# A second level of block products in the gates of a feed-forward layer

## The chip, the cores and the metric

One kernel on one core of a Trainium2 chip. TensorE (PE; PEld is its weight load), the Vector engine (DVE), ScalarE (ACT), GpSimd (POOL) and the queue engine SyncE (SP) run beside each other and wait for one another by semaphores. The metric is the device time of one execution in microseconds, as the median of several runs.

## What is computed

A decoder layer in f32 on x of 2×512 tokens with 1024 features: a state-space mixer with its own MLP, an attention-like product with quantized codes, and a feed-forward layer. The change is in the feed-forward layer:

```python
def _binary_diff_weight(w, base):
    d = w - base
    coeff = jnp.mean(jnp.abs(d))
    return base + coeff * jnp.sign(d)
W1 = _binary_diff_weight(w1, mean_w1)
W2 = _binary_diff_weight(w2, mean_w2)
W3 = _binary_diff_weight(w3, mean_w3)
gate = jnp.einsum('bsh,ih->bsi', hidden_states, W1)
up = jnp.einsum('bsh,ih->bsi', hidden_states, W3)
h = jax.nn.silu(gate) * up
return jnp.einsum('bsi,hi->bsh', h, W2)
...
x = x + _L0_ffn_ref(_layernorm(x, axis=-1), ...)
```
hidden_states is 1024 tokens × 1024, W1 and W3 are 3584×1024, W2 is 1024×3584.

## The kernel before

Products of matrices are made with seven block products instead of eight (Winograd's form of Strassen's method). For the gates the 3584 rows are cut into 14 groups of 256, and a group is two blocks of 128 rows (of features that come out), two blocks of 512 input features, and two blocks of 512 tokens. A block product is four matmuls of 128×128 weights by 512 tokens. `weight_blocks` makes the left-hand sums of a group's weight (four DVE instructions: s3, a sum in place of a21, s2, s4), `act_blocks` the right-hand ones (t2, t3, t4 and one in place), once for the layer. A `BlockProduct` then runs, for gate or up, on four PSUM banks a to d:

- product 1 into a; ACT copies it to p1
- product 6 into b; DVE: u2 = p1 + b
- product 5 into c, product 4 into d, product 7 onto b; DVE: u3 = p1 + b, c22 = u3 + c
- product 2 onto a (c11); DVE: u3 = u3 + d
- product 3 onto c; DVE: u2 = u2 + c

The four results are the blocks of the group's output. `gates` (L656) runs the groups in turn: gate's product, ACT's Silu of its four blocks, up's product, four DVE multiplications into the hidden tile h, four DVE sums of h's blocks (`hidden_blocks`), one store of h to DRAM (`fhd`). h has one buffer (`hp=1`). The W2 part of a group is brought beside that: `down_blocks` makes four sums in the tile t8 (`fw` in the trace), which is stored too (`fwd`). After the gates, `down` (L712) runs the last projection as seven products over those stores, with 256-column matmuls, and adds to the residual rows (`pairs`, four tiles of 1 MB in SBUF). The small loads `f1a`, `f1b` and so on are its operands; some of them are issued while the gates still run.

W1, W2 and W3 are built on the fly: `ffn_weight` (L1013) loads the sign tile (bf16, SP), ACT scales it (L1029), and a DMA from POOL's queue adds the base to it in SBUF (L1030), three times per group. Signs have been written by an earlier stage. The gates' weights have two buffers, used by odd and even groups.

Groups 0 and 1 begin early: products 1 and 2 of both (`first_products`, L635) need only the first 512 tokens, so `in_turn` puts them between the steps that finish the last 512 tokens (`codes`, `turned`, `product`, `normed`).

The order of the instructions on each engine is fixed when the program is built: a scheduler places them by its own estimate of times, within the bounds of the dependencies; `tc.issue_after(x)` keeps instructions behind x. Each engine runs its own list in order. SP and POOL issue the DMAs, and an issue that has to wait holds up those behind it on that queue.

Of the kernel before, what the change touches and what calls it, by code (L numbers as in the profile page):

```python
# [17 lines left out]
P = 128  # L18
NB = 2
L = 512  # L20
# [17 lines left out]
def decoder(ctx, tc, a, out):  # L38
# [141 lines left out]
    def tiles_waited(**kw):  # L180
        return tc.tile_pool(reuse_waits="tile", **kw)
# [9 lines left out]
    def add(out_, x, y):  # L191
        nc.vector.tensor_tensor(out_, x, y, ALU.add)  # L192

    def sub(out_, x, y):
        nc.vector.tensor_tensor(out_, x, y, ALU.subtract)  # L195
# [28 lines left out]
    def bank(k, name, shape=(P, 512)):  # L224
        return psum.tile(list(shape), F32, tag=f"k{k}", name=name)

    class BlockProduct:


        def __init__(self, places, pl, name, A, B):  # L230
            self.places, self.pl, self.name, self.A, self.B = places, pl, name, A, B
            self.banks = {}
            self.kept = None

        def mm(self, x, i, onto=False):
            if x not in self.banks:
# [18 lines left out]
        def others(self, then=lambda: None):  # L255
            ps = self.banks
            u2, u3, c22 = (self.t(x) for x in ("u2", "u3", "c22"))
            self.mm("b", 6)
            add(u2, self.p1, ps["b"])
            self.mm("c", 5)  # L260
            self.mm("d", 4)
            self.mm("b", 7, True)
            add(u3, self.p1, ps["b"])
            add(c22, u3, ps["c"])
            then()
            add(u3, u3, ps["d"])
            self.mm("c", 3, True)
            self.last = nc.vector.tensor_tensor(u2, u2, ps["c"], ALU.add).ins
            return self.kept if self.kept is not None else ps["a"], u2, u3, c22

        def whole(self):
            self.begin()
# [362 lines left out]
    def first_products(name, act, pl, i, gw, uw):  # L635

        first = {1: act[0][:, :4, :], 2: act[0][:, 4:, :]}
        both = []
        for odd, (x, w) in enumerate((("g", gw), ("u", uw))):
            places = (odd, 2 + odd, 4 + odd, 6 + odd)  # L640
            p = BlockProduct(places, pl, f"{name}{x}{i}", {1: w[:, :4, :P], 2: w[:, 4:, :P]}, first)
            p.weight = w
            if i:
                p.places, p.pl = (2 + 2 * odd,), {"p1": pl["p1b"]}
            both.append(p)

        def c11(p, odd):
            p.c11()
            if i:
                p.kept = pl["c1"].tile([P, L], F32, tag="c", name=f"{p.name}k")  # L650
                nc.scalar.copy(p.kept, p.banks.pop("a"))
                p.places, p.pl = (odd, 2 + odd, 4 + odd, 6 + odd), pl

        return both, [p.begin for p in both] + [lambda p=p, o=o: c11(p, o) for o, p in enumerate(both)]

    def gates(name, act, acts, g, pl, weights, side, begun):  # L656


        dram = [
            [tc.dram_tile([P, 7, 512], F32, name=f"{name}{x}d{i}") for i in range(NG)] for x in ("h", "w")  # L660
        ]
        with g:
            B = act_blocks(name, act, [pl["ap"].tile([P, 4, L], F32, tag=f"t{i}", name=f"{name}t{i}") for i in (2, 3, 4)])
            for i in range(NG):
                gw, uw, t8 = weights(i)
                if i in begun:
# [19 lines left out]
                if not callable(t8):  # L686
                    down_weights(t8, gate.last)
                elif last:
                    down_weights(t8(contexts[0].last), gate.last)
                sg = [gate.t("s")] + list(gc[1:])  # L690
                for o, c in zip(sg, gc):
                    silu = nc.scalar.activation(o, c, AF.Silu).ins
                side(i, pl.get("raw"))
                uc = up.others() if i in begun else up.whole()
                if callable(t8) and not last:
                    down_weights(t8(silu), up.last)
                h = pl["hp"].tile([P, 7, L], F32, tag="h", name=f"{name}h{i}")
                for slot, s_, u_ in zip((0, 3, 1, 2), sg, uc):
                    nc.vector.tensor_tensor(h[:, slot, :], s_, u_, ALU.mult)
# [10 lines left out]
    H, Q = NG // 2, 256  # L710

    def down(name, dram, space, places, finish, work):  # L712

# [141 lines left out]
            ctx_codes(i // 4, i % 4)  # L855

    loaded = [mlp_weights(0)]
    begun, steps = first_products("m", h2T, pl, 0, *loaded[0][:2])
    for step in steps:
        step()  # L860
    dram = gates("m", h2T, acts, g, pl, lambda i: loaded.pop() if loaded else mlp_weights(i), abs_sums, {0: begun})


# [139 lines left out]
                pending.pop(0)()  # L1003

    down("m", dram, 512, (0, 1, 7, 3, 6, 5, 2, 8, 4, 9, 10, 11), ready, work)
    x3T.append(acts.enter_context(tiles_waited(name="x3b", bufs=1)).tile([P, KC, L], F32, name="x3T1"))

    g = ExitStack()
    pl = open_pools(g, "f", ("p1b", "c1", "sp", "ap", "p1", "hp", "t8"))
    g.enter_context(tiles_waited(name="fgap1", bufs=1)).tile([P, 256], F32, name="fgap1")  # L1010
    pl.update(open_pools(g, "f", ("w", "w1")))

    def ffn_weight(i, j, after=None):  # L1013

        n, base = FFN[j]
        if n == "w2":
            to = pl["t8"].tile([P, 8, 512], F32, tag="t8", name=f"fw2{i}")
            dst = to[:, :4, :].rearrange("p a b -> p (a b)")
        else:
            to = pl[("w", "w1")[i % 2]].tile([P, KC, GW], F32, tag="w", name=f"f{n}{i}")  # L1020
            dst = flat(to)
        if "sign" in pl:
            src = pl["sign"].tile([P, KC * GW], BF16, tag="sign", name=f"fs{n}{i}")
# [7 lines left out]
        return to  # L1031

    early = [[ffn_weight(i, j) for j in (0, 1)] for i in (0, 1)]
    traced = nc.cur_bb.bb.instructions
    last = {}

    def in_turn(*parts):
# [9 lines left out]
        return got_  # L1047

    ctx1 = contexts[1]
    begun0, first0 = first_products("f", x3T, pl, 0, *early[0])  # L1050
    begun1, first1 = first_products("f", x3T, pl, 1, *early[1])
    for t in (6, 7):
        ctx1.codes(t)
    in_turn(*first0)
# [4 lines left out]
    pl.update(open_pools(g, "f", ("tmp", "sign")))  # L1059
# [65 lines left out]
```

## Time and profile before

| what | us |
|---|---|
| median of 3 runs | 2484.68 (2483.78 to 2493.46) |
| the profiled execution, its time | 2487.05 |
| its span | 2485.3 |
| first products of groups 0 and 1 begin | 1494.3 |
| their second-stage products begin | 1538.2 |
| gates end, last projection begins | 2184.2 |
| one group of gates | 48.07 |

The span is the time from the first to the last instruction on the core; what lies around it is not in the trace. The profile's page gives busy times by engine; the trace can be asked for the instructions in order of time (the timeline), for stretches of time with the busy time of each engine, and for DMA issues with their time to landing. A matmul's recorded length contains the time for its results to come out, so that neighbours overlap: their pace is read from the distance of their starts. One f32 matmul is two instructions of PE in the trace.

In the gates of this layer the DMA engines are busy 66% of the time at 181 GB/s, ACT 9.2 us and POOL 2.6 us of a group's 48.07.

### The profile page before, as it was taken

To read this page: it belongs to the slowest core of one execution; us is meant where nothing else is said; L and a number is where in the kernel's file an instruction comes from. 1 tells how busy PE (TensorE), PEld (TensorE's weight loads), DVE (VectorE), ACT (ScalarE), POOL (GpSimd) and SP (SyncE) were. 2 spreads that over 40 slices of the span, in tenths; PEclk is the share of its full clock that TensorE was granted. 3 is DMA by queue.
4 is the path that set the end of the run, shared out by engine and by line. 5 is a ranking of instruction groups with operands and counts; after the bars stand their busy time and mean duration, and the time that the engine had idled before them with its cause. 6 is when DMAs were issued, how large, how long until landed. Compare 5 with 4: busy or idle time off the path is not lost.

```text
span 2485.3 us, 20211 instructions
## 1 busy us (share of the span) xinstructions
PE 2438.6 (98%) x7484; PEld 1371.2 (55%) x7492; DVE 1300.0 (52%) x1949; ACT 563.7 (23%) x674; POOL 315.7 (13%) x166
## 2 busy tenths in 40 slices
PE   7999999899999999999999999999999999999999
PEld 5445444444444444445888784444444444488888
DVE  4656676554645556444655654533443343365554
ACT  3222243443324333310000323222112112100000
POOL 1002020522323323210000110000000000000000
PEclk9999999899999999999999999999999999999999
DMA  3110032688888887876856450867576666575651
GB/s 137 36 50 19 28 123 85 241 338 326 337 313 323 350 324 318 324 255 204 249 148 185 134 148 18 217 201 188 151 212 169 163 183 181 165 241 163 210 165 64
DMA packets 174626, 477.50 MB, mean 192 GB/s; under 512 B 20416, under 2 KB 124864, under 8 KB 143552
## 3 DMA queue, kind: packets, MB, share of 16 engines
q1 hardware_dynamic: 167904, 427.98, 47.9%
q0 software_dynamic: 6624, 48.24, 9.9%
q8 instruction: 59, 0.97, 0.2%
q14 instruction: 39, 0.32, 0.0%
HBM read 340.87 MB, written 133.17 MB: 191 GB/s over the span
## 4 chain that ended last, share of the span: by engine, by line
PE 80%; DMA 7%; POOL 4%; DVE 4%; ACT 2%; issue 2%; SPq 1%; POOLq 0%; DVEq 0%; ACTq 0%
DMA smean_w<-in_mean_w 6%; POOL sw L849 3%; PE op L565 2%; ACT sgw L851 1%; PE xa L949 1%; PE dps L349 1%; PE y L485 1%; PE cb L477 1%; DVE down L195 0%; DVE hid L192 0%; PE fo1c L745 0%; PE mo4c L745 0%; PE fo7a L745 0%; PE fo2a L745 0%; PE mo5a L745 0%
## 5 line engine op out<-in xcount | busy, mean ns | idle before, releaser
L849 POOL TENSOR_TENSOR sw<-sw,smean_w 128x2048 f32<-128x2048 f32 x42 | 197.8, 4710 | 403.6 <-DMA smean_w<-in_mean_w 403.6
L851 ACT ACTIVATE sgw<-sw 128x2048 bf16<-128x2048 f32 x42 | 80.2, 1910 | 334.6 <-POOL sw L849 332.1
L1029 ACT ACTIVATE fw<-fsw,coeff 128x2048 f32<-128x2048 bf16 x38 | 75.9, 1997 | 216.7 <-DMA fsw<-sign 45.6
L1030 POOL DMA_DIRECT2D fw<-in_mean_w x42 | 36.2, 861 | 598.7 <-ACT fw L1029 582.8
L853 ACT ACTIVATE sw<-sw 128x2048 f32<-128x2048 f32 x42 | 80.1, 1908 | 0.9
L195 DVE TENSOR_TENSOR down<-down 128x512 f32<-128x512 f32 x56 | 77.6, 1406 | 0.7
L511 POOL TENSOR_TENSOR mz<-mz,ys 128x512 f32<-128x512 f32 x16 | 20.7, 1293 | 309.4 <-DVE ys L508 277.3
L565 PE MATMUL op<-wout,mz 128*128 128x512 f32 x128 | 56.6, 592 | 0.0
L91 POOL TENSOR_TENSOR q_r<-q_e,mhalf 128x1 f32<-128x1 f32 x8 | 6.5, 807 | 259.7 <-DVE q_e L87 259.1
L565 PEld LDWEIGHTS op<-wout,mz 128*128 128x128 f32 x128 | 23.9, 190 | 27.7 <-issue 27.5
L195 DVE TENSOR_TENSOR fw<-fw 128x512 f32<-128x512 f32 x56 | 37.1, 683 | 0.1
L118 PE MATMUL h1T<-ident,h 128*128 128x128 f32 x64 | 15.2, 383 | 16.6 <-ACT h L340 10.7
L195 DVE TENSOR_TENSOR mh<-mh 128x512 f32<-128x512 f32 x42 | 28.8, 686 | 0.5
L195 DVE TENSOR_TENSOR fh<-fh 128x512 f32<-128x512 f32 x42 | 28.7, 682 | 0.1
L949 PE MATMUL xa<-c,c1T 128*128 128x512 bf16 x122 | 28.1, 379 | 0.5 <-ACT c1T L937 0.2
L192 DVE TENSOR_TENSOR hid<-hid,op 128x512 f32<-128x512 f32 x24 | 15.9, 683 | 23.8 <-PE op L565 23.8
L349 PEld LDWEIGHTS dps<-wdt,h1T 128*128 128x128 f32 x128 | 23.7, 272 | 2.4 <-issue 1.8
L161 ACT ACTIVATE cc<-ctx,back 128x2048 bf16<-128x2048 f32 x8 | 16.0, 1996 | 27.1 <-DVE ctx L160 27.1
L349 PE MATMUL dps<-wdt,h1T 128*128 128x8 f32 x128 | 22.1, 301 | 0.0
L584 POOL TENSOR_TENSOR hid<-hid,xa 128x1024 f32<-128x1024 f32 x8 | 20.4, 2558 | 11.7 <-DMA xa<-in_x 9.1
L118 PEld LDWEIGHTS h1T<-ident,h 128*128 128x128 f32 x64 | 12.1, 223 | 17.1 <-ACT h L340 10.7
L952 DVE SCALAR_TENSOR_TENSOR hid<-xa,s,hid 128x512 f32<-128x512 f32 x16 | 12.0, 749 | 17.8 <-PE xa L949 17.7
(1979 smaller groups left out, 5300.8 us busy)
## 6 DMA issues: line engine op xcount, KB each, us to landing
sw<-in_w SPq DMA_DIRECT2D x42, 1024.0 KB, 7.7
smean_w<-in_mean_w SPq DMA_DIRECT2D x42, 1024.0 KB, 9.2
fw<-in_mean_w POOLq DMA_DIRECT2D x42, 1024.0 KB, 10.6
mwd<-down SPq DMA_DIRECT2D x14, 1792.0 KB, 7.2
fwd<-fw SPq DMA_DIRECT2D x14, 1792.0 KB, 8.9
mhd<-mh SPq DMA_DIRECT2D x13, 1792.0 KB, 7.0
fhd<-fh SPq DMA_DIRECT2D x13, 1792.0 KB, 10.3
sign<-sgw SPq DMA_DIRECT2D x42, 512.0 KB, 3.0
```

Source lines behind the costliest of these rows:

```text
L118: nc.tensor.transpose(ps[:, i, :], src[:, k * P : (k + 1) * P], ident)
L195: nc.vector.tensor_tensor(out_, x, y, ALU.subtract)
L349: nc.tensor.matmul(dps[:, t, :], h1T[t // TPB][:, k, c : c + P], wdt[:, k, :], start=(k == 0), stop=(k == KC - 1))
L477: nc.tensor.matmul(cb, o["B"][:, cols], o["C"][:, :, cols], start=True, stop=True)
L485: nc.tensor.matmul(y, o["xt"][:, c, :], att, start=True, stop=(c == 0))
L565: nc.tensor.matmul(ps, A[p][:, k, t * P : t * P + P], B[p][:, k, :], start=(k == 0), stop=(k == 3))
L849: nc.gpsimd.tensor_tensor(w, w, b, ALU.subtract)
L851: nc.scalar.activation(sg, w, AF.Sign)
L853: nc.scalar.activation(w, w, AF.Abs, accum_out=sums[:, j, i : i + 1])
L949: nc.tensor.matmul(ps, self.c1T[:, k, c : c + P], self.c2[k // 4][:, k % 4, hs], start=(k == 0), stop=(k == KC - 1))
L1029: nc.scalar.activation(dst, src, AF.Identity, scale=coeff[:, j : j + 1])
L1030: nc.gpsimd.dma_start(dst, a[base][i].rearrange("p a b -> p (a b)"), accum_op=ALU.add)
```

## The change

Products 1 and 2 of gate and up share their right-hand sides, and so do 6 and 7. Gate and up are now taken as two row blocks of one product, the 512 input features as 2×256 and the 512 tokens as 2×256, and the same seven-product form is applied once more inside (`second_level`). One call does two of the outer products together: an index q of 2 stands for product 1 and 2 (or 6 and 7), whose results lie beside each other in one bank. Each inner product is four matmuls of 256 columns. The sums for the inner level are made by `second_level_right` (once per layer and pair) and `second_level_left` (per group and pair). The outer products 3, 4 and 5 stay as they were (`one`), for gate and up.

The combination of the outer products is done by additions over gate and up together, on results in SBUF. Groups 0 and 1 take products 1 and 2 in the plain form (`first_two`), as these begin early. The tiles for the right-hand sums of the inner level (`places`, three of 1 MB) and for the signs take the place of the residual rows, which are written to DRAM (`xd`) before the gates and read back (`xf`) after them.

```diff
-    POOLS = dict(t8=1, w=2, w1=2, raw=2, ap=1, sp=2, hp=1, tmp=7, p1=2, p1b=2, c1=2, sign=2)
+    POOLS = dict(t8=1, w=2, w1=2, raw=2, ap=1, sp=2, hp=1, tmp=7, p1=2, o12=2, o67=1, px=2, s23=1, s4=2, y12=1, y67=1)
...
+    def second_level_right(b, t2, t3, t4):
+        b11, b12, b21, b22 = (b[:, :, k : k + 2, c : c + Q] for k in (0, 2) for c in (0, Q))
+        sub(t3, b22, b12)
+        sub(b12, b12, b11)
+        sub(t2, b22, b12)
+        sub(t4, b21, t2)
+        return {1: b11, 2: b21, 3: b22, 4: t4, 5: b12, 6: t2, 7: t3}
+
+    def second_level_left(g_, u_, s1, s2, s3, s4):
+        a11, a12, a21, a22 = g_[:, :, :2], g_[:, :, 2:], u_[:, :, :2], u_[:, :, 2:]
+        sub(s3, a11, a21)
+        add(s1, a21, a22)
+        sub(s2, s1, a11)
+        sub(s4, a12, s2)
+        return {1: a11, 2: a12, 3: s4, 4: a22, 5: s1, 6: s2, 7: s3}
+
+    def second_level(name, banks, p1, A, B, O):
+        ps = {x: bank(k, f"{name}{x}", (P, 2, Q)) for x, k in zip("abcd", banks)}
+        def mm(x, i, onto=False):
+            for q in range(2):
+                for k in range(2):
+                    nc.tensor.matmul(
+                        ps[x][:, q, :], A[i][:, q, k, :], B[i][:, q, k, :],
+                        start=not onto and q == 0 and k == 0, stop=k == 1, skip_group_check=onto or q > 0,
+                    )
+        c11, u2, u3, c22 = (O[:, :, x, c : c + Q] for x in (0, 1) for c in (0, Q))
+        mm("a", 1)
+        nc.scalar.copy(p1, ps["a"])
+        mm("b", 6)
+        add(u2, p1, ps["b"])
+        mm("c", 5)
+        mm("d", 4)
+        mm("b", 7, True)
+        add(u3, p1, ps["b"])
+        add(c22, u3, ps["c"])
+        mm("a", 2, True)
+        nc.scalar.copy(c11, ps["a"])
+        add(u3, u3, ps["d"])
+        mm("c", 3, True)
+        add(u2, u2, ps["c"])
...
+            for i in range(NG):
...
+                if i in begun:
+                    O12 = begun[i]
+                else:
+                    O12 = pl["o12"].tile([P, 2, 2, L], F32, tag="o", name=f"{name}o12_{i}")
+                    p1 = pl["px"].tile([P, 2, Q], F32, tag="p", name=f"{name}p12_{i}")
+                    second_level(f"{name}m{i}", X, p1, A12, B12, O12)
+                    add(O12[:, 1], O12[:, 0], O12[:, 1])
+                w2 = t8(None)
+                if i == 0:
+                    c, d = one("c", 5), one("d", 4)
+                p1 = pl["px"].tile([P, 2, Q], F32, tag="p", name=f"{name}p67_{i}")
+                O67 = pl["o67"].tile([P, 2, 2, L], F32, tag="o", name=f"{name}o67_{i}")
+                second_level(f"{name}n{i}", Y, p1, A67, B67, O67)
+                add(O67[:, 0], O12[:, 0], O67[:, 0])
+                turn = nc.vector.tensor_tensor(O67[:, 1], O67[:, 0], O67[:, 1], ALU.add).ins
+                if i:
+                    c = one("c", 5)
+                for j in range(2):
+                    add(O12[:, 0, j], O67[:, 1, j], c[j])
+                if i:
+                    d = one("d", 4)
+                for j in range(2):
+                    add(O67[:, 1, j], O67[:, 1, j], d[j])
+                one("c", 3, True)
+                coming.pop(0)
+                if not last:
+                    with tc.issue_after(turn):
+                        if i + 1 not in begun:
+                            A12 = outer_left(i + 1, *coming[0][:2])
+                        A, A67 = left(i + 1, *coming[0][:2])
+                if i == 0:
+                    b = act[0].rearrange("p (q k) l -> p q k l", q=2)
+                    B12 = second_level_right(b, ex[1][:, 1], ex[2][:, 0], ex[2][:, 1])
+                if i + 2 < NG:
+                    coming.append(weights(i + 2))
+                with tc.issue_after(turn):
+                    down_blocks(w2)
+                nc.sync.dma_start(dram[1][i], w2[:, 1:, :])
+                for j in range(2):
+                    add(O67[:, 0, j], O67[:, 0, j], c[j])
+                h = pl["hp"].tile([P, 7, L], F32, tag="h", name=f"{name}h{i}")
+                for slot, o in ((0, O12[:, 1]), (2, O12[:, 0]), (1, O67[:, 1]), (3, O67[:, 0])):
+                    nc.scalar.activation(o[:, 0], o[:, 0], AF.Silu)
+                    nc.vector.tensor_tensor(h[:, slot, :], o[:, 0], o[:, 1], ALU.mult)
...
+    xd = tc.dram_tile([P, NT // 2, 2 * D], F32, name="xd")
+    places = []
+    for j in range(NT // 2):
+        with tc.issue_after(loads):
+            nc.sync.dma_start(xd[:, j, :], flat(pairs[j]))
+        if j < 3:
+            places.append(xpool.tile([P, 2, D], F32, tag=f"x{2 * j}", name=f"ft{j}"))
+        else:
+            two = xpool.tile([P, 2, KC * GW], BF16, tag=f"x{2 * j}", name="fsign")
+            sign_places.extend(two[:, k, :] for k in range(2))
...
-    dram = gates("f", x3T, acts, g, pl, ffn_weights, lambda i, wp: None, {0: begun0, 1: begun1})
-    down("f", dram, 14464, (9, 10, 11, 3, 0, 1, 4, 2, 5, 6, 7, 8), store, lambda: None)
+    dram = gates2("f", x3T, acts, g, pl, ffn_weights, {0: begun0, 1: begun1}, places)
+    for j in range(NT // 2):
+        pairs[j] = xpool.tile([P, 2, D], F32, tag=f"x{2 * j}", name=f"xf{2 * j}")
+        nc.sync.dma_start(flat(pairs[j]), xd[:, j, :])
+    down("f", dram, 14336, (9, 10, 11, 4, 2, 3, 5, 8, 0, 1, 6, 7), store, lambda: None)
```
`left` makes the outer sums of a group's weights, as `weight_blocks` did, and from them the inner ones of 6 and 7 (3 sums in one new tile and one in place); `outer_left` makes the inner sums of 1 and 2. L832 of the changed kernel is the addition called `turn`. `loads` is the last load that the first `down` issues on SP.

More of the change, by code (lines that the diff above doesn't have):

```diff
@@ L232, in __init__ @@
             self.banks = {}
-            self.kept = None
         def mm(self, x, i, onto=False):
@@ L268, in others @@
             self.last = nc.vector.tensor_tensor(u2, u2, ps["c"], ALU.add).ins
-            return self.kept if self.kept is not None else ps["a"], u2, u3, c22
+            return ps["a"], u2, u3, c22
         def whole(self):
@@ L633, in open_pools, with first_products @@
         return pl
-    def first_products(name, act, pl, i, gw, uw):
+    def first_products(name, act, pl, gw, uw):
         first = {1: act[0][:, :4, :], 2: act[0][:, 4:, :]}
@@ L639, in first_products @@
         for odd, (x, w) in enumerate((("g", gw), ("u", uw))):
-            places = (odd, 2 + odd, 4 + odd, 6 + odd)
-            p = BlockProduct(places, pl, f"{name}{x}{i}", {1: w[:, :4, :P], 2: w[:, 4:, :P]}, first)
+            p = BlockProduct((odd, 2 + odd, 4 + odd, 6 + odd), pl, f"{name}{x}0", {1: w[:, :4, :P], 2: w[:, 4:, :P]}, first)
             p.weight = w
-            if i:
-                p.places, p.pl = (2 + 2 * odd,), {"p1": pl["p1b"]}
             both.append(p)
-        def c11(p, odd):
+        for p in both:
+            p.begin()
+        for p in both:
             p.c11()
[L649 to L654, printed above, removed]
+        return both
     def gates(name, act, acts, g, pl, weights, side, begun):
@@ L684, in down_weights @@
                     nc.sync.dma_start(dram[1][i], t8[:, 1:, :])
[L686 to L689, printed above, removed]
+                down_weights(t8, gate.last)
                 sg = [gate.t("s")] + list(gc[1:])
                 for o, c in zip(sg, gc):
-                    silu = nc.scalar.activation(o, c, AF.Silu).ins
-                side(i, pl.get("raw"))
+                    nc.scalar.activation(o, c, AF.Silu)
+                side(i, pl["raw"])
                 uc = up.others() if i in begun else up.whole()
-                if callable(t8) and not last:
-                    down_weights(t8(silu), up.last)
                 h = pl["hp"].tile([P, 7, L], F32, tag="h", name=f"{name}h{i}")
@@ new lines, in first_two, with step @@
+    def first_two(name, act, pl, i, gw, uw, banks):
+        O = pl["o12"].tile([P, 2, 2, L], F32, tag="o", name=f"{name}o12_{i}")
+        ps = []
+        def step(p, x, w):
+            if not p:
+                ps.append(bank(banks[x], f"{name}a{x}_{i}"))
+            for k in range(4):
+                nc.tensor.matmul(
+                    ps[x], w[:, 4 * p + k, :P], act[0][:, 4 * p + k, :],
+                    start=not p and k == 0, stop=k == 3, skip_group_check=p > 0,
+                )
+            nc.scalar.copy(O[:, p, x, :], ps[x])
+        return O, [lambda p=p, x=x, w=w: step(p, x, w) for p in range(2) for x, w in enumerate((gw, uw))]
@@ new lines, in gates2, with outer_left, left, one @@
+    def gates2(name, act, acts, g, pl, weights, begun, places):
+        dram = [
+            [tc.dram_tile([P, 7, 512], F32, name=f"{name}{x}d{i}") for i in range(NG)] for x in ("h", "w")
+        ]
+        with g:
+            t23 = pl["ap"].tile([P, 2, 4, L], F32, tag="t23", name=f"{name}t23")
+            t4 = pl["ap"].tile([P, 4, L], F32, tag="t4", name=f"{name}t4")
+            B = act_blocks(name, act, (t23[:, 0], t23[:, 1], t4))
+            ex = [x.rearrange("p a (b c d) -> p a b c d", b=2, c=2) for x in places]
+            B67 = second_level_right(t23, ex[0][:, 0], ex[0][:, 1], ex[1][:, 0])
+            B12 = None
+            def outer_left(i, gw, uw):
+                y = pl["y12"].tile([P, 4, 2, 2, P], F32, tag="y", name=f"{name}y12_{i}")
+                gv, uv = (w[:, :, :P].rearrange("p (q k) c -> p q k c", q=2) for w in (gw, uw))
+                return second_level_left(gv, uv, *(y[:, j] for j in range(4)))
+            def left(i, gw, uw):
+                s23, A = [], []
+                for x, w in (("g", gw), ("u", uw)):
+                    a11, a12, a21, a22 = (w[:, k : k + 4, c : c + P] for c in (0, P) for k in (0, 4))
+                    two = pl["s23"].tile([P, 2, 4, P], F32, tag=x, name=f"{name}{x}{i}s")
+                    four = pl["s4"].tile([P, 4, P], F32, tag=x, name=f"{name}{x}{i}s4")
+                    sub(two[:, 1], a11, a21)
+                    add(a21, a21, a22)
+                    sub(two[:, 0], a21, a11)
+                    sub(four, a12, two[:, 0])
+                    s23.append(two)
+                    A.append({3: four, 4: a22, 5: a21})
+                y = pl["y67"].tile([P, 3, 2, 2, P], F32, tag="y", name=f"{name}y67_{i}")
+                return A, second_level_left(s23[0], s23[1], s23[1][:, :, :2], *(y[:, j] for j in range(3)))
+            coming = [weights(0), weights(1)]
+            A, A67 = left(0, *coming[0][:2])
+            for i in range(NG):
+                t8 = coming[0][2]
+                last = i == NG - 1
+                X, Y = ((0, 1, 2, 3), (4, 5, 6, 7))[:: 1 if i % 2 else -1]
+                def one(x, p, onto=False, into={}):
+                    if not onto:
+                        into[x] = [bank(X["ccdd".index(x) + j], f"{name}{i}{x}{j}") for j in range(2)]
+                    for j in range(2):
+                        for k in range(4):
+                            nc.tensor.matmul(
+                                into[x][j], A[j][p][:, k, :], B[p][:, k, :],
+                                start=not onto and k == 0, stop=k == 3, skip_group_check=onto,
+                            )
+                    return into[x]
+                if i in begun:
[36 more added lines that the diff above has]
+                nc.sync.dma_start(dram[1][i], w2[:, 1:, :])
+                for j in range(2):
+                    add(O67[:, 0, j], O67[:, 0, j], c[j])
[3 more added lines that the diff above has]
+                    nc.vector.tensor_tensor(h[:, slot, :], o[:, 0], o[:, 1], ALU.mult)
+                if last:
+                    nc.sync.dma_start(dram[0][i][:, :3, :], h[:, :3, :])
+                hidden_blocks(h)
+                if last:
+                    nc.sync.dma_start(dram[0][i][:, 3:, :], h[:, 3:, :])
+                else:
+                    nc.sync.dma_start(dram[0][i], h)
+        acts.close()
+        return dram
@@ L857, in decoder @@
     loaded = [mlp_weights(0)]
-    begun, steps = first_products("m", h2T, pl, 0, *loaded[0][:2])
-    for step in steps:
-        step()
+    begun = first_products("m", h2T, pl, *loaded[0][:2])
     dram = gates("m", h2T, acts, g, pl, lambda i: loaded.pop() if loaded else mlp_weights(i), abs_sums, {0: begun})
@@ L1005, in decoder @@
     down("m", dram, 512, (0, 1, 7, 3, 6, 5, 2, 8, 4, 9, 10, 11), ready, work)
+    traced = nc.cur_bb.bb.instructions
+    loads = [ins for ins in traced if ins.engine == mybir.EngineType.SP][-1]
     x3T.append(acts.enter_context(tiles_waited(name="x3b", bufs=1)).tile([P, KC, L], F32, name="x3T1"))
     g = ExitStack()
-    pl = open_pools(g, "f", ("p1b", "c1", "sp", "ap", "p1", "hp", "t8"))
-    g.enter_context(tiles_waited(name="fgap1", bufs=1)).tile([P, 256], F32, name="fgap1")
-    pl.update(open_pools(g, "f", ("w", "w1")))
+    pl = open_pools(g, "f", ("o12", "o67", "px", "s23", "s4", "y12", "y67", "ap", "w", "w1"))
     def ffn_weight(i, j, after=None):
@@ L1021, in ffn_weight @@
             dst = flat(to)
-        if "sign" in pl:
-            src = pl["sign"].tile([P, KC * GW], BF16, tag="sign", name=f"fs{n}{i}")
+        if sign_places:
+            src = sign_places[0]
+            sign_places.reverse()
             nc.sync.dma_start(src, signs[j][i])
@@ L1031, in ffn_weight @@
         return to
+    sign_places = []
     early = [[ffn_weight(i, j) for j in (0, 1)] for i in (0, 1)]
-    traced = nc.cur_bb.bb.instructions
     last = {}
@@ L1049, in decoder @@
     ctx1 = contexts[1]
-    begun0, first0 = first_products("f", x3T, pl, 0, *early[0])
-    begun1, first1 = first_products("f", x3T, pl, 1, *early[1])
+    begun0, first0 = first_two("f", x3T, pl, 0, *early[0], (0, 1))
+    begun1, first1 = first_two("f", x3T, pl, 1, *early[1], (2, 4))
     for t in (6, 7):
@@ L1058, in decoder @@
     q.close()
-    pl.update(open_pools(g, "f", ("tmp", "sign")))
+    pl.update(open_pools(g, "f", ("hp", "t8")))
+    xd = tc.dram_tile([P, NT // 2, 2 * D], F32, name="xd")
[5 more added lines that the diff above has]
+            places.append(xpool.tile([P, 2, D], F32, tag=f"x{2 * j}", name=f"ft{j}"))
+        else:
+            two = xpool.tile([P, 2, KC * GW], BF16, tag=f"x{2 * j}", name="fsign")
+            sign_places.extend(two[:, k, :] for k in range(2))
     def ffn_weights(i):
```

## The prediction

> **What bounds the kernel now.** I read the busy times first, then TensorE (PE) over one group of the feed-forward gates, then the Vector engine (DVE) beside it, then the stages before and after.
>
> The page's busy times, and one group of gates between two of its first matmuls (columns: stretch, length, then busy us and count of PE, PEld, DVE, ACT, POOL, then the granted clock, DMA share and GB/s):
>
> ```profile
> PE 2438.6 (98%) x7484; PEld 1371.2 (55%) x7492; DVE 1300.0 (52%) x1949; ACT 563.7 (23%) x674; POOL 315.7 (13%) x166
> ```
> ```profile
> 1751.60:1799.67 48.07, 48.07 (x114) 21.29 (x113) 19.18 (x30) 9.22 (x9) 2.58 (x4) 1.00 0.66 181
> ```
> PE has no gap at full clock; DVE is busy 19.2 of 48.1 us with 30 instructions. From the start of group 0's second-stage products (1538.21) to the end of group 13 (2184.17) PE takes 645.96 us, against 645.5 for 80 + 12×56 matmuls at the spacing below. So a matmul less is time less, as long as DVE keeps up. The spacing is in the timeline of PE (start, us, what; one 4-step product is 8 instructions):
>
> ```profile
> 1751.57 3.60 PE L239 MATMUL fg5a<-x3T,fw 128*128 128x512 f32 x8
> ...
> 1799.64 0.59 PE L239 MATMUL fg6a<-x3T,fw 128*128 128x512 f32 x1
> ...
> 2226.66 6.21 PE L745 MATMUL fo6a<-f6b,f6a 128*128 128x256 f32 x28
> 2232.70 6.21 PE L745 MATMUL fo6b<-fw6e,fh6e 128*128 128x256 f32 x28
> ```
> 48.07/56 = 0.8584 us for a 512-column f32 matmul, 6.045/14 = 0.4316 for a 256-column one: half the columns cost half plus 2.4 ns, and PEld keeps pace.
>
> The pace of dependent DVE work, in the timeline of group 0 (a product's second use of its bank b, then u3, c22, then the matmul onto bank c):
>
> ```profile
> 1551.95 1.88 PE L239 MATMUL fu0b<-ft,fu0s 128*128 128x512 f32 x4
> 1552.15 0.69 DVE L192 TENSOR_TENSOR fg0u<-fg0p,fg0b 128x512 f32<-128x512 f32 x1 [9.61 <-PE fg0b L239]
> 1552.87 0.69 DVE L192 TENSOR_TENSOR fg0c<-fg0u,fg0c 128x512 f32<-128x512 f32 x1
> 1553.47 0.68 DVE L699 TENSOR_TENSOR fh<-fg0s,fu0a 128x512 f32<-128x512 f32 x1
> 1553.66 0.64 PE L239 MATMUL fg0c<-x3T,fg0s 128*128 128x512 f32 x1
> ```
> DVE starts follow each other by 0.60 us, or 0.72 where one reads the last one's result. From the end of b's streaming (1551.95) to the next matmul on c is 1.71 us, and PE filled just that with other matmuls. Two transfers matter (median us to landing):
>
> ```profile
> fwd<-fw SPq DMA_DIRECT2D x14, 1792.0 KB, 8.9
> fhd<-fh SPq DMA_DIRECT2D x13, 1792.0 KB, 10.3
> ```
>
> **What the Trainium skill says.** "TensorE: Matmul & The Clock Gate", section "Wait — 56ns, not 53.3ns?": a matmul costs its columns plus some 2.5 ns; the trace agrees (2.4 ns per f32 matmul instruction: 0.8584/2 = 429.2 and 0.4316/2 = 215.8 ns). "VectorE: DVE Perf Modes", section "The perf-mode tier table": an f32 tensor_tensor has one rate, from SBUF or PSUM; here both take 0.68 us at 128x512, and a 1024-wide one 1.28 (the f32 L192 pairs and L939). "SBUF — State Buffer", section "SBUF: two separate sides": a DVE instruction with two SBUF inputs and a GpSimd one that reads SBUF lock each other out; the trace agrees where GpSimd subtracts (L195 `down` 1406 ns, against 683 for `fw`), and in these gates GpSimd only issues DMAs. "DMA: Bandwidth & Descriptors", section "Queues, rings and completion order": within one engine's ring descriptors are taken in order; no view here tests it.
>
> **The change, part by part.**
>
> 1. *Products 1 with 2, and 6 with 7.* Each pair for gate and up is 16 matmuls of 512 = 13.734 us; it becomes 7×4 = 28 of 256 = 12.085. Saved 1.65. The second pair in 14 groups, the first in 12 (groups 0 and 1 keep the plain form): 26×1.65 = **−42.9 us**. A full group becomes 28+28 short and 24 long: 24.17 + 20.60 = 44.77 instead of 48.07.
>
> 2. *DVE per group.* In the changed order: 2×5 bank additions, 6 with the c and d banks, 4+8+4 weight sums, 4 for `down_blocks`, 8 for h, and three 1024-wide: 44×0.64 (19.18/30) + 3×1.28 = 32.0 us of 44.8. It fits in sum. Position by position, with 0 at a group's first matmul: the last bank of the 6,7 pair ends at 24.17, the three additions after it (L832 last) at 27.7. Then 24 additions and the rest stand ahead of the next group's u2, as the 33rd. u2 must end 6.9 us into the next group (four short products: 1.73 each), at 51.7. So 33 instructions have 24.0 us, 0.727 each; they take 0.60 to 0.72. Slack 0 to 4 us: no stall. ACT has 10.7 us of work and is not late.
>
> 3. *Bank c.* The last product onto c stands one product (1.726 us) after b's; the chain u3, c22 needs 1.71. A tie: 0 per occurrence, at worst 0.3 if the strided 2x256 tiles or a wake-up cost more; 24 occurrences. I take 0.05: **+1.2**. Nothing covers it if the chain grows: what is late then is PE itself.
>
> 4. *Hidden tile.* h has one buffer: the first product of a group (DVE, just ahead of the 6,7 pair's u2) waits for the store of the last h. The store goes out at about 5.3 us, lands at 14 to 16, and u2 is due at 18.3. In groups 8 to 13, SP has in front of it an early load of `f1b` that waits for the store of `fw`, issued at about 43 of the group before, after a sign load that waits for ACT: it lands at about 7.5, h goes at 8, lands at 15 to 18.3. Loss 0 to 1.5 in six groups; I take 0.2 each: **+1.2**.
>
> 5. *Start.* Six 1024-wide sums for the right side, two groups' weight sums and the first h fall in groups 0 to 2. Laying DVE's order against PE's with the spacings above, groups 0 and 1 lose some 0.7 us and group 2's u2 comes 0.8 late, its c 0.2: **+2** (0 to 5). The products begun in between fill the same holes as before.
>
> 6. *Residual rows.* Four 1 MB writes on SP, behind the last loads of the first down projection. Those were late already: DVE waits for them at 1463.39 (4.56 us, `m4b`). The writes are queued behind them on the same queue, so I take 0; if they shared evenly, 2 MB at the 225 GB/s moved there is 9 us. The reads back: two wait for the last 6,7 pair, 20.6 us before the gates end; 2 MB at 200 to 300 GB/s has landed 10 us before the end. The adders of the rows come 20 us after. **0**.
>
> 7. *The seam.* Before, the first down product starts at 2184.17 without a gap. Now SP holds three chunks of a11 and all of b11 behind the first store of the last h, which needs the d banks and a Silu: at about 5.3 us before the end. Ten issues of 0.47 put the last at −0.3, landed (2.0 to 4.1) at +2 to +4, wanted at +2.6: 0.5 lost. DVE still owes h one product and two sums before b12: ready at +6.9 instead of 6.04, 0.9 more; product 6, now third, needs s2 at about +14.2 where PE is at 13: 1.2. **+2.6** (0.5 to 8 if the loads crowd).
>
> Sum: −42.9 + 1.2 + 1.2 + 2 + 0 + 2.6 = −35.9. The profiled execution's span of 2485.3 becomes 2449.4; it took 2487.05, 2.4 above the median of 2484.68. Against the median: **2448.8**.
>
> **Rivals.**
>
> *A, DVE trails a little.* If its 33 instructions take 0.77 each, u2 is 1.4 us late: 12×1.4 = 17, 2466. For it: 71% busy, in strict order, many dependent pairs. Against: 0.72 is the slowest spacing seen here.
>
> *B, the seam costs more.* The reads back, the last stores and some 80 small loads share one queue; first loads 12 us later give 2461. For it: landings of 18.1 us for 128 KB loads where the queues were full (`m4b`). Against: at the old seam small loads landed in 2 to 4, and nothing big is in flight 10 us before the end.
>
> *C, slower.* DVE becomes the bound: the same 33 instructions, in each full group. From 0.82 us each (33×0.82 − 24 = 3.06, times 12 = 36) the gain is gone; at 0.90 each, 5.7×12 = 68 gives 2517. That would take the 1.4 us instructions of the other gates stage, if GpSimd's weight DMAs (L1030, three a group, 0.86 us) blocked DVE as its subtractions do. Against: with the same DMAs DVE runs at 683 ns in these gates now.
>
> **How the numbers follow.** Forecast 0.70, own range 2442 (parts 3 to 7 all free) to 2462 (their worse values, some together). A 0.13, B 0.07, C 0.06, and 0.04 for a loss at the start or by the residual writes that leaves no visible change. Range 2440 to 2467 leaves out C, most of that last case and the top of A. Beyond ±0.5% (12.4 us), which this measurement can tell from no change: faster 0.90, same 0.04, slower 0.06.
>
> **What would show it.** Full groups of 44.8 to 45.2 us; PE idle ahead of the last product onto c by at most 0.1; 47 DVE instructions per group, at 0.68 for 512 wide; 2 us of PE idle in groups 0 to 2; 2 to 3 in the first 20 us of the last projection, which is otherwise unchanged. It is wrong if u2 is what PE waits for in steady groups (A, C), if `m4b` lands later, or if PE stands at the seam for over 6 us (B).

## The result, and the profile after

| | before | after |
|---|---|---|
| median of 8 runs each | 2489.02 (2483.78 to 2494.14) | 2478.56 (2472.04 to 2485.85) |
| ratio | | 0.9956 (95% interval 0.9939 to 0.9974) |
| the profiled execution, its span | 2485.3 | 2476.8 |

The change gains 0.4%, 10.5 us between the medians; 35.9 were forecast. PE's busy time fell by 29.7 us, in more instructions than before, as they are shorter. The page's first line after (before: PE 2438.6 in 7484 instructions, DVE 1300.0):

```profile
PE 2408.9 (97%) x8116; PEld 1490.0 (60%) x8116; DVE 1465.2 (59%) x2175; ACT 583.0 (24%) x704; POOL 313.8 (13%) x166
```

Where the gain went is seen in the groups. The trace after by stretches, group 6, and then groups 8 to 12 (each from one first matmul to the next; columns as in the view of before: stretch, length, busy us and count of PE, PEld, DVE, ACT, POOL, granted clock, DMA share, GB/s):

```profile
1792.00:1837.10 45.10, 45.10 (x161) 30.15 (x160) 31.34 (x47) 10.55 (x11) 2.58 (x3) 1.00 0.66 184
```
```profile
1882.80:1932.70 49.90, 46.83 (x162) 31.42 (x161) 31.34 (x47) 10.55 (x11) 2.56 (x3) 0.97 0.62 172
1932.70:1981.10 48.40, 45.09 (x162) 30.12 (x161) 31.33 (x47) 10.55 (x11) 2.58 (x3) 1.00 0.64 173
1981.10:2031.30 50.20, 46.73 (x161) 31.41 (x160) 31.34 (x47) 10.55 (x11) 2.59 (x3) 0.97 0.63 170
2031.30:2082.40 51.10, 47.99 (x161) 32.29 (x160) 31.34 (x47) 10.55 (x11) 2.57 (x3) 0.93 0.62 172
2082.40:2128.90 46.50, 45.10 (x161) 30.15 (x160) 31.34 (x47) 6.65 (x9) 0.86 (x1) 1.00 0.59 179
```
A full group takes 45.1 us with no idle, as forecast: 48.07 before. In groups 8 to 12 the same instructions take 246.1 us, 20.6 more than five times 45.1. Length less busy PE is idle: 3.07, 3.31, 3.47, 3.11 and 1.40, together 14.4. The other 6.2 us are busy time above 45.1, in the three groups whose granted clock is below 1.

Against the span of before, the 8.5 us come together so: the stages ahead of the second down projection's fourth product, whose code is unchanged, +5.6; from there to the gates +2.0; gates −18.0 (645.96 to 627.92); from the end of the gates to the first matmul of product 6 of the last projection +1.9; the rest 0. The first term is no part of the change: that product begins at 1443.9 us in the one profile of before, and at 1447.1 to 1453.5 in the profiles of the changed kernel and of the runs below. In the traces of before and after, DVE, ACT, POOL and SP run the same instructions in the same order up to there.

Group 8 in the order of time, after. The queues first, POOL's and then SP's (start us, us, what):

```profile
1875.13 0.85 POOL L1189 DMA_DIRECT2D fw<-in_mean_w  x1 [20.74 <-ACT fw L1188]
1878.56 0.85 POOL L1189 DMA_DIRECT2D fw<-in_mean_w  x1 [2.58 <-ACT fw L1188]
```
```profile
1879.55 0.32 SPq L855 DMA_DIRECT2D fwd<-fw  x1
1896.54 0.32 SPq L894 DMA_DIRECT2D f1b<-fwd  x1
1896.91 0.42 SPq L868 DMA_DIRECT2D fhd<-fh  x1
```
Two base transfers of 1 MB start, then the store of the W2 sums (`fwd`). The early load `f1b` reads what that store wrote, so SP issues it only when the store has landed, 17 us later. The hidden tile's store (`fhd`) stands behind it on SP and leaves 14.1 us into the group. Now DVE and PE:

```profile
1899.09 1.23 DVE L192 TENSOR_TENSOR fo<-fo 128x1024 f32<-128x1024 f32 x1 [3.25 <-ACT fo L743]
1903.75 0.69 DVE L861 TENSOR_TENSOR fh<-fo 128x512 f32<-128x512 f32 x1 [3.44 <-DMA fhd<-fh]
1904.36 0.68 DVE L192 TENSOR_TENSOR fo<-fp,fn8b 128x512 f32<-128x512 f32 x1
```
```profile
1900.13 1.89 PE L727 MATMUL fn8d<-ft,fu8s 128*128 128x256 f32 x8
1905.09 3.00 PE L727 MATMUL fn8b<-ft,fy 128*128 128x256 f32 x8 [3.07 <-DVE fo L192]
1907.89 2.61 PE L727 MATMUL fn8a<-ft,fg8s 128*128 128x256 f32 x8
```
The first multiplication into the one hidden tile (L861) waits for the landing of its last store. u2, right behind it, is what PE waits for. After that idle time the next two lines of eight matmul instructions take 3.00 and 2.61 us where 1.89 is usual.

The same trace also holds a second suspect. ACT waits too for the landing of `fwd`, since the scaling of W2 writes the one tile `t8`, and it holds the copy of c11 (L743) behind it, for which DVE waits 3.25 us:

```profile
1896.58 2.00 ACT L1188 ACTIVATE fw<-fsign,coeff 128x2048 f32<-128x2048 bf16 x1 [11.24 <-DMA fwd<-fw]
1898.49 0.57 ACT L743 COPY fo<-fm8a 128x512 f32<-128x512 f32 x1
```

### The profile page after: what moved, and what is told of

Read it like the earlier page. It is cut to its first block, busy times and chain, and to the rows that moved or that the text cites. A ratio compares the mean times of both kernels' runs of the same rounds, so it can differ in the third digit from the quotient of the medians.

```text
span 2476.8 us, 21784 instructions
## 1 busy us (share of the span) xinstructions
PE 2408.9 (97%) x8116; PEld 1490.0 (60%) x8116; DVE 1465.2 (59%) x2175; ACT 583.0 (24%) x704; POOL 313.8 (13%) x166
## 4 chain that ended last, share of the span: by engine, by line
PE 75%; DMA 10%; DVE 7%; POOL 3%; ACT 2%; issue 2%; SPq 1%; POOLq 0%; DVEq 0%; ACTq 0%
DMA smean_w<-in_mean_w 4%; PE op L564 3%; DMA fwd<-fw 3%; POOL sw L1009 2%; DMA fhd<-fh 2%; DVE fo L192 1%; DMA up<-in_up_w 1%; ACT sgw L1011 1%; PE xa L1107 1%; PE dps L348 1%; PE fa L757 1%; DVE fy L195 1%; PE y L484 1%; DVE down L195 1%; PE f0c L812 1%
## 5 line engine op out<-in xcount | busy, mean ns | idle before, releaser
L1188 ACT ACTIVATE fw<-fsign,coeff 128x2048 f32<-128x2048 bf16 x38 | 76.1, 2004 | 200.2 <-DMA fwd<-fw 118.2
L860 ACT ACTIVATE fo<-fo 128x512 f32<-128x512 f32 x56 | 35.1, 627 | 148.7 <-DVE fo L192 148.6
L861 DVE TENSOR_TENSOR fh<-fo 128x512 f32<-128x512 f32 x56 | 37.2, 690 | 26.7 <-DMA fhd<-fh 21.0
L195 DVE TENSOR_TENSOR fw<-fw 128x512 f32<-128x512 f32 x56 | 38.5, 687 | 0.1
L192 DVE TENSOR_TENSOR fo<-fo 128x1024 f32<-128x1024 f32 x12 | 14.7, 1225 | 30.0 <-ACT fo L743 29.8
L757 PE MATMUL fa<-x3T,fw 128*128 128x512 f32 x64 | 30.1, 624 | 2.1 <-ACT fo L761 2.1
## 6 DMA issues: line engine op xcount, KB each, us to landing
fwd<-fw SPq DMA_DIRECT2D x14, 1792.0 KB, 16.6
```

The lines of the kernel that those rows point to most:

```text
L757: nc.tensor.matmul(ps[x], w[:, 4 * p + k, :P], act[0][:, 4 * p + k, :], start=not p and k == 0, stop=k == 3, skip_group_check=p > 0,)
L861: nc.vector.tensor_tensor(h[:, slot, :], o[:, 0], o[:, 1], ALU.mult)
```

## The experiments

Theory 1: the place of the early load on SP, ahead of the hidden tile's store, together with a store that lands in 17 us. Theory 2: ACT, held by the scaling of W2. Theory 3: DVE trails by itself, rival A of the prediction. Before had medians of 2490.5 to 2493.2 us beside these runs, and 2489.0 beside the changed kernel, so rows are best compared by their ratios.

| run | median us | ratio to before | start of gates to first f6 product, us |
|---|---|---|---|
| before | | | 688.5 |
| after | 2478.56 | 0.9956 (0.9939 to 0.9974) | 672.3 |
| e_hold | 2470.78 | 0.9915 (0.9900 to 0.9929) | 661.4 |
| e_act | 2478.84 | 0.9949 (0.9934 to 0.9965) | 670.9 |
| e_base | 2551.39 | 1.0243 (1.0227 to 1.0259) | 743.9 |
| e_both | 2559.78 | 1.0274 (1.0257 to 1.0291) | 755.6 |
| e_add | 2499.42 | 1.0028 (1.0015 to 1.0042) | 691.2 |
| b_act | 2463.68 | 0.9874 (0.9857 to 0.9891) | 653.6 |
| b_head | 2457.71 | 0.9848 (0.9834 to 0.9863) | 652.5 |
| b_base1 | 2467.54 | 0.9885 (0.9870 to 0.9899) | 663.4 |
| e_noread | 2454.40 | 0.9856 (0.9839 to 0.9874) | 651.4 |

The last column is from one profile each. The stages ahead differ by some us from one execution to the next, and it leaves them out.

### Early loads behind the hidden tile's store (e_hold)

```diff
-                    nc.sync.dma_start(dram[0][i], h)
+                    stores.append(nc.sync.dma_start(dram[0][i], h).ins)
...
                     for c in range(H):
-                        nc.sync.dma_start(tl[:, c, :], dr[c][...])
+                        with tc.issue_after(stores[halves[x] * H + c]) if stores and not n else nullcontext():
+                            nc.sync.dma_start(tl[:, c, :], dr[c][...])
```
`halves[x]` is the half of the 14 groups that the operand comes from.

> The early loads f1b, one per group from group 7 on, are queued on SP behind the hidden tile's store of the same group instead of ahead of it; nothing else moves. Theory 1 (the early load waits on SP for the landing of the fw store, 17 us, and holds the hidden tile's store, so the one hidden tile comes free late): groups 8 to 12 fall from 46.5-51.1 us to 45.1-45.7, the time by 18 to 20 us to about 2459, ratio to the kernel before about 0.988; PE waits before fn8b to fn12b fall from 14.4 us together to under 3. Theory 2 (ACT, held by the scaling of w2 until the fw store has landed, delays the copies that DVE needs): ACT still waits for the same landing, so at least 15 of the 20 us stay, time 2474 to 2479. Theory 3 (DVE simply trails): under 3 us gained.

Groups 8 to 12 took 45.0, 46.1, 44.9, 46.0 and 46.3 us, 228.2 in place of 246.1: 17.9 gained there. Group 8 now, and SP beside it:

```profile
1880.40:1925.40 45.00, 45.00 (x162) 30.17 (x161) 31.35 (x47) 10.55 (x11) 2.56 (x3) 1.00 0.67 189
```
```profile
1877.16 0.32 SPq L855 DMA_DIRECT2D fwd<-fw  x1
1885.52 0.32 SPq L868 DMA_DIRECT2D fhd<-fh  x1
1895.72 0.32 SPq L1187 DMA_DIRECT2D fsign<-sign  x1
1896.14 0.37 SPq L898 DMA_DIRECT2D f1b<-fwd  x1
```
The store goes out 5.1 us into the group, not 14.1, though `fwd` lands as late as before. Not all of it came through: PE's longest wait here is a new one, at the last projection's start.

```profile
PE fo1a L909 <- issue: 5.7, 1, 5.7
...
PE fn6b L727 <- DVE fo L192: 1.3, 1, 1.3
PE fn12b L727 <- DVE fo L192: 1.1, 1, 1.1
```
The edit also held group 13's early load behind the very last store. With that idle time the stretch from the first f1 product to the first f6 product took 51.0 us in place of 43.9, which gave back 7.1 us. The last column of the table fell by 10.9 us, and by the ratios the gain is 0.4%, about 10 us, where 18 to 20 were expected. The mechanism and its size in groups 8 to 12 are theory 1's; 2 and 3 fall as causes of these 18 us.

### W2's scaling behind the copy of c11 (e_act)

```diff
-                w2 = t8(None)
+                w2 = t8(copied)
```
`copied` is ACT's copy of c11 in the first pair's `second_level`.

> The scaling of w2 stands on ACT behind the copy of c11 of the pair 1, 2 instead of ahead of it; the early loads stay ahead of the hidden tile's store. Theory 1: the hidden tile's store still leaves at the landing of the fw store, so the multiplication into the hidden tile still starts about 21 us into groups 8 to 12; 0 to 2 us gained, time 2476 to 2479. Theory 2: the copy leaves some 5 us earlier and the add behind it no longer waits, groups 8 to 12 fall to 45-47 us, 12 to 20 us gained. Theory 3: under 1 us.

ACT's wait for `fwd` in groups 6 to 12 fell from 77.0 us to 14.7. PE's waits stayed (us in all, times, longest):

```profile
PE fn10b L727 <- DVE fo L192: 3.3, 1, 3.3
PE fn9b L727 <- DVE fo L192: 3.2, 1, 3.2
PE fn8b L727 <- DVE fo L192: 2.9, 1, 2.9
PE fn11b L727 <- DVE fo L192: 2.8, 1, 2.8
```
Groups 8 to 12 took 244.1 us, 2 less than in the changed kernel. So ACT's long wait, the larger number in the profile, cost next to nothing as long as the hidden tile's store was late.

### Base transfers behind the last Silu (e_base, e_both)

```diff
-                if i + 2 < NG:
-                    coming.append(weights(i + 2))
                 with tc.issue_after(turn):
                     down_blocks(w2)
...
+                if i + 2 < NG:
+                    coming.append(weights(i + 2, silu))
```
`silu` is the group's last Silu; both weights' scalings, and so their base transfers, come behind it. e_both has the edit of e_hold as well.

> Sign loads, scalings and the two 1 MB base transfers of the gate and up weights of group i+2 are issued behind the last Silu of the group, some 15 us later, so that they no longer start just ahead of the fw store; the early loads stay ahead of the hidden tile's store. Theory 1 with its first half right (the fw store lands in 17 us because it shares the DMA engines with these transfers): fw store's median landing falls from 16.6 to 8-10 us, the hidden tile's store leaves 6 to 8 us earlier, groups 8 to 12 fall to 45-46.5 us, 15 to 20 us gained, about 2460. If the landing stays at 15 us or more for another reason, theory 1 and 2 both expect no gain. Theory 3: under 3 us gained.

The landing time fell, further than expected, and the gain did not come: the run is 73 us slower than the changed kernel. The page's DMA part (KB each, median us to landing):

```profile
fwd<-fw SPq DMA_DIRECT2D x14, 1792.0 KB, 5.9
...
fhd<-fh SPq DMA_DIRECT2D x13, 1792.0 KB, 18.1
```
`fwd` lands in 5.9 us now and the hidden tile's store in 18.1; in the changed kernel it was 16.6 and 8.2. The transfers that slowed one store now slow the other, in every group up to 12. Group 6 of this run, DVE:

```profile
1854.69 0.69 DVE L859 TENSOR_TENSOR fh<-fo 128x512 f32<-128x512 f32 x1 [8.96 <-DMA fhd<-fh]
```
It is the same late multiplication, 23.3 us into a group that took 53.2, reached by another way. I had priced the move by what it does for the store it leaves and not by the store it meets.

> Both edits: early loads behind the hidden tile's store, and the base transfers behind the last Silu. Theory 1: as the first edit alone, with at most 3 us more (group 7 and what is left of the waits for ACT): 2456 to 2459. Theory 2: only the later transfers help, so no more than that edit alone. A third outcome: the later transfers land too late for the next groups, and PE waits for the left sides; then it is slower than the first edit alone.

Holding the early loads as well changed nothing for the better: 2559.78. Here the queue's order no longer matters, since the store's own landing is late.

### The wait added where it was not (e_add)

```diff
+                    if i < H:
+                        nc.sync.dma_start(pl["sk"].tile([P, Q], F32, tag="sk", name=f"{name}sk{i}"), dram[1][i][:, 4, Q:])
                     nc.sync.dma_start(dram[0][i], h)
```

> The changed kernel with the suspected wait added where it was not: in groups 0 to 6 a 128 KB load of the group's own fw store is queued on SP ahead of the hidden tile's store (into a scratch tile that nobody reads; from group 4 on it stands ahead of the store, before that behind it). Theory 1 (this place in the queue is the cause): groups 5, 6 and 7, which ran in 45.1, 45.1 and 45.7 us, go to 48 to 51 each, time 9 to 15 us longer than the changed kernel's, about 2490. Theory 2 (ACT's wait is the cause): ACT's order and waits are unchanged, so 0 to 2 us.

The added load stood ahead of the hidden tile's store from the first one on, not only from group 4. SP around the start of group 3:

```profile
1654.98 0.32 SPq L855 DMA_DIRECT2D fwd<-fw  x1
1671.22 0.32 SPq L869 DMA_DIRECT2D fsk<-fwd  x1
1671.59 0.42 SPq L870 DMA_DIRECT2D fhd<-fh  x1
```
Groups 3 to 7 took 47.6, 47.7, 50.1, 48.7 and 47.9 us where the changed kernel took 45.1 four times and 45.7: +15.8, and PE waits for u2 in each. Groups 5 and 6 lie in the expected 48 to 51, group 7 just under it; 3 and 4 were not expected to lose. Groups 8 to 12 are 3.1 us longer too, and by the ratios the run is some 18 us slower than the changed kernel, where 9 to 15 were expected. The longest of PE's waits, in old and new places:

```profile
PE fn11b L727 <- DVE fo L192: 3.7, 1, 3.7
PE fn6b L727 <- DVE fo L192: 3.6, 1, 3.6
...
PE fn5b L727 <- DVE fo L192: 3.3, 1, 3.3
```
So the load in front of the store can be taken away and put elsewhere, and the loss follows it.

### Both holds, and the seam left as it was (b_act)

```diff
-... if stores and not n else nullcontext():
+... if stores and not n and halves[x] * H + c < NG - 1 else nullcontext():
```
The lines are against e_hold's; e_act's edit stands beside them.

> Early loads behind the hidden tile's store as in the first experiment, but not in group 13, whose last load now goes out as before; and the scaling of w2 behind the copy of c11. The last projection's start falls from an idle of 5.7 us to under 1.5. If ACT's wait for the fw store is what was left in groups 8 to 12 after the first edit, PE's waits before fn6b to fn12b (4.2 us there) fall under 1.5 and the time to 2461 to 2464; if the hidden tile's own store, landing in 12.3 us, is what was left, they stay at 3 to 4 us and the time is about 2465.

PE's waits before fn6b to fn12b fell to 0.9 us in all, and the seam's to 1.6. By itself this run says that what was left after e_hold was ACT. The traces don't bear that out. The lines below are the first multiplication into the hidden tile, in groups 6 and 11 of e_hold and in group 10 of b_head, the next run, which has the same edit of ACT; in brackets stand DVE's idle time and what ended it:

```profile
1808.24 0.69 DVE L861 TENSOR_TENSOR fh<-fo 128x512 f32<-128x512 f32 x1 [1.93 <-DMA fhd<-fh]
2035.06 0.69 DVE L861 TENSOR_TENSOR fh<-fo 128x512 f32<-128x512 f32 x1 [0.69 <-ACT fo L860]
```
```profile
1989.13 0.69 DVE L863 TENSOR_TENSOR fh<-fo 128x512 f32<-128x512 f32 x1 [5.05 <-DMA fhd<-fh]
```
Of the four groups of e_hold in which PE still waits, 6 and 9 wait for the hidden tile's store. In 11 and 12 ACT's Silu comes last, but the store had landed only 0.3 us earlier. In b_head PE waits 2.3 us again before fn9b to fn12b, behind that store each time. So theory 2 holds for a few tenths of a us in a group, and most of what was left is the store itself, which takes 12 to 14 us to land. Why it landed sooner in b_act is open.

### One copy on DVE (b_head)

```diff
-            nc.scalar.copy(O[:, p, x, :], ps[x])
+            (nc.scalar.copy if p or i or not x else nc.vector.tensor_copy)(O[:, p, x, :], ps[x])
```

> As the run before it, and one of the copies of the begun products of group 0 (the up half's first step) on DVE instead of ACT. If the 2.1 us that PE waits at the start of the stage come from ACT's order (the copy stands behind the codes of t = 6 and 7), the wait falls under 0.5 us and the time by 1.5 to 2 us against that run; if DVE is as late as ACT there, nothing.

In the changed kernel's timeline of PE the begun products hold a wait for ACT, which is busy with the codes of t = 6 and 7, and eight slow matmul instructions after it; in this run all 32 go through in one piece:

```profile
1512.63 5.40 PE L757 MATMUL fa<-x3T,fw 128*128 128x512 f32 x8 [2.06 <-ACT fo L761]
```
```profile
1502.43 13.90 PE L758 MATMUL fa<-x3T,fw 128*128 128x512 f32 x32
```
Usual for eight is 3.60. From the fourth product of the down projection to the gates this run took 92.4 us, the changed kernel 96.4: 4.0 gained where 1.5 to 2 were expected, the wait and the slow matmuls behind it (the medians lie 6.0 apart). This is the fastest version that computes the whole layer, 1.5% under before. Its ratio of 0.9848 comes near what the prediction's own numbers make (2448.8/2484.68 = 0.9856): with the early load behind the store the gates take 608.4 us, where the sum made 607.5 (645.96 less the 38.5 of parts 1 to 5). The 2.0 us by which the stretch ahead of them lies under before's 94.4 are in no step, and are luck as far as the forecast goes.

### One base transfer on each side (b_base1)

```diff
+                if i + 2 < NG:
+                    coming[-1][1:1] = [ffn_weight(i + 2, 1, silu)]
```

> As the run before it, and the up weight's scaling and 1 MB base transfer of group i+2 behind the last Silu, so that one of the two large transfers starts ahead of the fw store and one behind the hidden tile's store. If a store that shares the engines with two such transfers lands in 16 to 18 us and one with none in 6 to 9, each store now shares with about one: both land in 10 to 13 us, no store is late for its reader, and the time is within 3 us of that run. If the last transfer collides with the hidden tile's store as both did when both were moved, its landing goes above 15 us and the time up by 20 us or more.

```profile
fwd<-fw SPq DMA_DIRECT2D x14, 1792.0 KB, 12.1
...
fhd<-fh SPq DMA_DIRECT2D x13, 1792.0 KB, 12.8
```
The landings come out even, as expected, and groups 3 to 12 run as in b_head. The time is 9.8 us longer because of group 2, 55.8 us for 45.3, where PE waits 6.2 us for DVE. The trace names the chain, and it is the same one (POOL, SP, then DVE):

```profile
1620.53 0.87 POOL L1197 DMA_DIRECT2D fw<-in_mean_w  x1 [18.49 <-ACT fw L1196]
1624.82 0.86 POOL L1197 DMA_DIRECT2D fw<-in_mean_w  x1 [3.42 <-DVE fh L195]
```
```profile
1624.57 0.32 SPq L872 DMA_DIRECT2D fhd<-fh  x1
```
```profile
1639.08 0.69 DVE L863 TENSOR_TENSOR fh<-fo 128x512 f32<-128x512 f32 x1 [9.24 <-DMA fhd<-fh]
```
In this group both transfers stand at the hidden tile's store, 4.0 us ahead and 0.3 behind; it lands after 14.4 us, in b_head after 8.1. No run moves the second transfer away in this group alone.

### Without the reads of the residual rows (e_noread)

```diff
-        nc.sync.dma_start(flat(pairs[j]), xd[:, j, :])
+        nc.gpsimd.memset(flat(pairs[j]), 0.0)
```

> The fastest version so far (early loads held, w2's scaling behind c11, one copy on DVE) without the reads back of the residual rows: the rows are set to zero by GpSimd instead, so the output lacks the residual. Point 6 of the prediction (the four 1 MB reads are off the path): within 1.5 us of that version, the last projection's first 44 us the same within 1. Rival (they crowd the seam's loads on SP and the engines): the stretch from the first f1 product to the first f6 product falls from 44 us to 41-42 and the time by 2 to 4 us.

Against b_head the median is 3.3 us lower, but before was 2.7 us lower beside it as well, and the ratios, 0.9856 and 0.9848, show no gain. From the first f1 product to the first f6 product both take 44.1 us, so the rival falls. The profiles differ by 1 us in the gates, which one profile each can't tell from chance.

## Why the prediction was wrong

Direction and mechanism were right, and the gain was forecast more than three times too large. One term of the sum carries it.

**Step 4, the hidden tile: the term that was mis-sized.** It named the chain, an early `f1b` load on SP in front of the hidden tile's store from group 8 on, and took 1.2 us for it, with 1.5 per group as the worst. It cost 20.6 us in groups 8 to 12, up to 6 a group. Two numbers failed. The first is the landing of `fw`'s store. It was put at 7.5 us into the group from the row of before, 8.9 us to landing; in group 8 it landed at 13.7, after 17.0. (The hidden tile's own store, 10.3 us in the profile of before, took 12.5 in groups 3 to 6.) The row of before was made with one base transfer ahead of the store (the nearest one 5.4 us ahead, the next 17 us behind). POOL and SP, before:

```profile
1846.88 0.87 POOL L1030 DMA_DIRECT2D fw<-in_mean_w  x1 [18.76 <-ACT fw L1029]
1869.50 0.86 POOL L1030 DMA_DIRECT2D fw<-in_mean_w  x1 [21.75 <-ACT fw L1029]
```
```profile
1852.23 0.32 SPq L684 DMA_DIRECT2D fwd<-fw  x1
```
The changed order puts both there, 4.4 and 1.0 us ahead. The step counted the place of the store in time and SP's order, and left out what POOL issues beside it. "DMA: Bandwidth & Descriptors", section "Queues, rings and completion order", in the Trainium skill says that a DMA engine takes turns between its queues packet by packet; the runs fit that without showing the turns themselves: the same 1792 KB store landed in 5.9 us (e_base), 12.1 (b_base1) or 16.6 (after) with neither, one or both of these transfers just ahead of it. The second number is what a wait costs: idle time alone was priced, and 6.2 of the 20.6 us are slow matmuls after it.

**Steps 1 and 2 held.** Steady groups took 45.1 us where 44.8 to 45.2 were forecast, with 47 DVE instructions and no idle time of PE. DVE took 31.34 us a group (32.0 forecast). Rival A, DVE trailing, fell: e_hold leaves DVE's work as it is, and group 8 has no idle time. Rival C fell with it; DVE's instructions kept their 0.68 to 0.69 us beside POOL's transfers.

**Step 3, bank c.** It held. Group 6 after, PE from the second pair's product 4 on:

```profile
1809.32 1.89 PE L727 MATMUL fn6d<-ft,fu6s 128*128 128x256 f32 x8
1811.20 1.99 PE L727 MATMUL fn6b<-ft,fy 128*128 128x256 f32 x8
1813.03 1.89 PE L727 MATMUL fn6a<-ft,fg6s 128*128 128x256 f32 x8
1814.76 1.93 PE L727 MATMUL fn6c<-ft,fy 128*128 128x256 f32 x8
1816.53 1.02 PE L812 MATMUL f6c<-x3T,fw 128*128 128x512 f32 x2
```
A product takes 1.73 us from start to start. The one onto c took 1.77, so 0.04 was lost, where 0.05 was taken; the first pair's took the same. A full group is still 0.35 us above the 44.77 of pure matmuls, and the other 0.26 lies at fn6b (1.88 and 1.83 us for 1.73), where PE needs u2: it comes a little late in groups 3 to 6 too. There the multiplication ahead of it starts at 17.9 us into the group, behind ACT's Silu and with the hidden tile's store landed 0.3 us earlier. Where it starts by 17.4, as in groups 4 and 5 of e_hold, a group takes 44.86 us. So this is a small part of step 4's loss.

**Step 5, the start.** It held for groups 0 to 2: groups 0 and 1 took 65.0 us for 64.5 of matmuls, group 2 took 45.8 for 44.8, so 1.5 was lost and 2 forecast. But a loss ahead of them, in products that were said to fill the same holes as before, is in no step: the second step of a begun product adds onto a bank that ACT still has to copy, and that cost 4.0 us (b_head). The stretch grew by 2.0 only, since before had slow matmuls of its own there (4.62 us for eight instructions at 1530.33), so the total came near by luck. No step named that copy's place behind the codes on ACT.

**Step 6, residual rows.** The reads cost nothing at the seam. The writes show no cost either: with ACT's wait gone, the stretch that holds them is 92.4 us against 94.4 before, and DVE's wait for `m4b`, the sign named for them, is 4.4 us after and 4.6 before. No run leaves them out.

**Step 7, the seam.** +1.9 us, 2.6 forecast. Rival B fell.

So 20.6 measured for 1.2 in step 4 explains 19 of the 27 us by which the profiled span missed its forecast, and the unchanged stages, 5.6 us shorter in the profile of before, most of the rest. Between the medians the starting point counts as well: the forecast took before at 2484.68, the median of three runs, and eight gave 2489.02.

## What to carry to other kernels

In these runs a store's time to landing depended on what else was in flight: before taking it from the old profile, list what every queue issues in the 20 us ahead of it, in the new order. A load queued in front of a store makes that store wait for everything the load waits for, and a tile with one buffer passes this on to the engine that refills it. When large transfers are moved out of one store's way, look for the store they will meet, or split them between the two.

## What the runs showed of the hardware

An idle time of PE can cost more than its length. After 3.07, 3.47 and 3.11 us of idle in groups 8, 10 and 11 the group's matmuls took 1.6 to 2.9 us longer at a granted clock of 0.93 to 0.97. After 3.31 us in group 9, and after 3.6 in group 6 of e_add, they did not (clock 1.00); after 2.06 us at the start they did (5.40 us for 3.60, at 0.67). "TensorE: Matmul & The Clock Gate", section "HAM oscillation — how this bites in real kernels", warns of idle gaps above about 3.4 us; gaps a little under that, and one of 2.06, were enough here, and one of 3.6 was not. The section "The HAM clock gate (the "warmup" mystery)" says the window in which activity is counted runs freely. That would fit gaps of one size which cost and don't cost, but no run here shows it.
